# Two graph layers on one core: storing the zeros of the first sums in 13 parts beside the first table

## The chip, the cores and the metric

The kernel runs on one core of a Trainium2 chip. The metric is device time in microseconds (us) of one execution; the time before is the median of 9 runs. The engines have short names: PE is TensorE (PEld its weight loads), DVE is VectorE, ACT is ScalarE, POOL is GpSimd, SP is SyncE. SP, ACT and POOL also issue DMAs; "ACTq" and "SPq" in the views are such issues.

## The reference, cut to what matters

There are 6250 nodes of 256 features and 100,000 edges sorted by destination. Four layers follow one another, each on the normalised output of the one before, each added to it:

```python
x = x + gat_gat(_layernorm(x), src, dst, ...)     # two attention layers over the edges
x = x + experts_top2(_layernorm(x), ...)          # 8 experts, two for each node
x = x + mean_of_neighbours(_layernorm(x), ...)    # weighted mean over the edges, then an MLP
x = x + experts_routed(_layernorm(x), ...)        # 8 experts, routed once for all nodes
```

Only the beginning is changed. The first attention layer needs, for every node, a table row of `z = _layernorm(x) @ W1` (two heads of 128) with the scores `el` and `er`; messages `z[src]`, weighted by a softmax over the edges of a destination, are then added up for each destination.

## The kernel before, in words

**Stages.** The first stage is the pool `g1` (lines 1145 to 1184). It makes `table1` (6250 rows of 262 numbers) and the lists of edges. The second stage (`gat_edges`, from line 1232) gathers rows of `table1` by edge and adds them up, 50 tiles of 125 nodes one after another. Between the two lies `gat_general` (line 1185), a loop for oversized tiles that runs zero times here, but whose entry every engine passes before the second stage begins.

**What runs in the first stage.** Three jobs are mixed, each instruction placed on its engine's queue by a scheduler when the program is built; an engine then executes its queue strictly in order.

- *Edge ranges* (`edge_ranges`): where each tile's edges begin. It is one long chain of small steps, most of them on DVE, with three round trips to memory by indirect DMAs on POOL: `part` (L177), `win` (L220, three) and `orec`/`ow` (L293, eight). It ends with `starts` (L383).
- *Edge lists* (`edge_lists`): seven groups of up to eight tiles. For each group SP loads `raw` (L460) and POOL loads `wraw` (L463), addressed by `starts`; DVE, ACT and PE turn them (L467 to L499), and SP stores `dl_d` (L480) and `run_d` (L495). `raw` and `wraw` have two buffers.
- *The table*: 13 blocks of four tiles (the last of two). For each block ACT issues the load of `xb` (L1153); DVE normalises it (`normalize`, L508 to L513); PE turns it (L523) and ACT empties that into `xT` (L524); for each of the four tiles PE multiplies by `wl` into one bank `pz` (L1164), ACT copies 256 columns of it into `rows` (L1168) and DVE the other four (L1171); DVE copies `er` out (L1172); ACT issues two stores to `table1` (`store_tiles`, L1106). `xb` has three buffers, `rows` and `pz` two each.

At the end `item_lists` (L413 to L433) makes the lists that the loop of `gat_general` would use: five rounds of two wide products on PE, DVE work between them, two small stores each.

**The zeros.** `sums1` (6528 rows of 258 numbers) must be zero before the second stage adds to it. `clear(nc.sync, sums1, 0, 1)` at L1183 does it in one DMA on SP's queue, from a tile of zeros; the scheduler places it early, as L1120 of the profile. The first reader of `sums1` in the second stage is L745, then L663.

Of the kernel before, what the change touches and what calls it, by code (L numbers as in the profile page):

```python
# [13 lines left out]
F32 = mybir.dt.float32  # L14
# [4 lines left out]
OP = mybir.AluOpType  # L19
# [8 lines left out]
P = 128  # L28
NP = 125
D = 256  # L30
# [4 lines left out]
TB = 4  # L35
# [9 lines left out]
def network(ctx: ExitStack, tc: tile.TileContext, a, out, n_nodes: int, n_edges: int):  # L45


    nc = tc.nc
# [7 lines left out]
    blocks = [(t, min(TB, NT - t)) for t in range(0, NT, TB)]  # L56
# [445 lines left out]
    def normalize(pool, outs, ins, keep=None):  # L502

        n, p = len(ins), ins[0].shape[0]
        mv = keep if keep is not None else pool.tile([P, TB, 2], F32, name="mv")
        for j, x in enumerate(ins):
            st = pool.tile([P, 6], F32, name="st", bufs=4)
            nc.vector.bn_stats(st[:p], x)  # L508
            nc.vector.bn_aggr(mv[:p, j, :], st[:p])
        nc.scalar.activation(mv[:p, :n, 1:2], mv[:p, :n, 1:2], AF.Sqrt, bias=eps[:p])  # L510
        nc.vector.reciprocal(mv[:p, :n, 1:2], mv[:p, :n, 1:2])
        for j, (o, x) in enumerate(zip(outs, ins)):
            nc.vector.tensor_scalar(  # L513
                o, x, mv[:p, j, 0:1], mv[:p, j, 1:2], op0=OP.subtract, op1=OP.mult
            )

    def transpose_to(xT, ps, ins, func=AF.Copy):

        n, q = len(ins), ins[0].shape[0]
        for k in range(KD):  # L520
            pt = ps.tile([P, TB, P], F32, name="pt")
            for j, x in enumerate(ins):
                nc.tensor.transpose(pt[:, j, :q], x[:, k * P : (k + 1) * P], identf[:q, :q])  # L523
            nc.scalar.activation(  # L524
                xT[:, k, : n * q].rearrange("p (j q) -> p j q", q=q), pt[:, :n, :q], func
            )


    def gat_width(H):
        return H * (D // H + 1)  # L530

    def gat_weights(pool, W, al, ar, H):

        d = D // H
        wl = pool.tile([P, KD, D + 2 * H], F32, name="wl")
        nc.sync.dma_start(wl[:, :, 0:D], W.rearrange("(k p) f -> p k f", p=P))
        for s, v in enumerate((al, ar)):
            vb = row_to_all(pool, v, f"vb{s}")
            for h in range(H):
                for k in range(KD):  # L540
                    pr = pool.tile([P, D], F32, name="pr", bufs=2)
                    nc.vector.tensor_mul(pr[:, :d], wl[:, k, h * d : (h + 1) * d], vb[:, h * d : (h + 1) * d])
                    nc.vector.tensor_reduce(
                        wl[:, k, D + s * H + h : D + s * H + h + 1], pr[:, :d], AX.X, OP.add
                    )
        return wl
# [550 lines left out]
    def tiles_of(src, t0, n):  # L1097

        w = src.shape[1]
        return bass.AP(tensor=src.tensor, offset=src.offset + t0 * NP * w, ap=[[w, P], [NP * w, n], [1, w]])  # L1100

    def store_tiles(queue, dst, t0, n, v):

        to = dst[t0 * NP : (t0 + n) * NP, :].rearrange("(j p) w -> p j w", p=NP)
        for q in (slice(0, NP // 16 * 16), slice(NP // 16 * 16, NP)):
            queue.dma_start(to[q], v[q])  # L1106
# [7 lines left out]
    def clear(queue, acc, part, parts):  # L1114

        w = acc.shape[1]
        step = -(-NS // parts)
        lo, hi = part * step, min(NS, (part + 1) * step)
        if lo < hi:
            queue.dma_start(  # L1120
                acc[:, :].rearrange("(p j) w -> p j w", p=P)[:, lo:hi, :],
                blank[:, 0:w].unsqueeze(1).to_broadcast([P, hi - lo, w]),
            )
# [12 lines left out]
    x5_d = dram.tile([NT * NP, D], F32, name="x5_d")  # L1136
    uv_d = dram.tile([NT * NP, 2 * D], F32, name="uv_d")
    x6_d = dram.tile([NT * NP, D], F32, name="x6_d")
    NS = -(-(NT * NP + 2 * P) // P)
    sums1 = dram.tile([NS * P, gat_width(2)], F32, name="sums1")  # L1140
    sums2 = dram.tile([NS * P, gat_width(1)], F32, name="sums2")
    sums3 = dram.tile([NS * P, D + 1], F32, name="sums3")


    with tc.tile_pool(name="g1w", bufs=1) as wpool, tc.tile_pool(name="g1", bufs=2) as work, tc.tile_pool(
        name="g1p", bufs=2, space=PSUM
    ) as ps:
        edge_ranges()
        edge_lists()
        wl = gat_weights(wpool, a["L0_gnn_W1"], a["L0_gnn_al1"], a["L0_gnn_ar1"], 2)  # L1150
        for t0, n in blocks:
            xb = work.tile([P, TB, D], F32, name="xb", bufs=3)
            nc.scalar.dma_start(xb[:, :n, :], tiles_of(a["x"], t0, n))  # L1153
            xb = xb[:NP]
            normalize(work, [xb[:, j, :] for j in range(n)], [xb[:, j, :] for j in range(n)])
            xT = work.tile([P, KD, TB * NP], F32, name="xT")
            transpose_to(xT, ps, [xb[:, j, :] for j in range(n)])
            rows = work.tile([NP, TB, D + 6], F32, name="rows")
            heads = rows[:, :, 0 : D + 2].rearrange("p j (h f) -> p j h f", h=2)
            nc.vector.memset(heads[:, :, :, 0:1], 1.0)  # L1160
            for j in range(n):
                pz = ps.tile([P, 512], F32, name="pz")
                for k in range(KD):
                    nc.tensor.matmul(  # L1164
                        pz[:NP, : D + 4], xT[:, k, j * NP : (j + 1) * NP], wl[:, k, :],
                        start=(k == 0), stop=(k == KD - 1),
                    )
                nc.scalar.copy(  # L1168
                    heads[:, j, :, 1:], pz[:NP, 0:D].rearrange("p (h f) -> p h f", h=2)
                )  # L1170
                nc.vector.tensor_copy(rows[:, j, D + 2 :], pz[:NP, D : D + 4])  # L1171
            nc.vector.tensor_copy(er1[:NP, t0 : t0 + n, :], rows[:, :n, D + 4 :])  # L1172
            store_tiles(nc.scalar, table1, t0, n, rows[:, :n, :])
        none = wpool.tile([NT + 1, 2 * P], BF16, name="none")
        nc.vector.memset(none, 0.0)
        for v, k in ((er1_d, 6), (er2_d, 3)):
            nc.sync.dma_start(
                v[:, :, CH:, :].rearrange("t k c e -> t k (c e)"),
                none.unsqueeze(1).to_broadcast([NT + 1, k, 2 * P]),
            )  # L1180
        nc.sync.dma_start(x2_d[NT * NP :, :], blank[: P - NP, 0:D])
        nc.sync.dma_start(table3[NT * NP :, :], blank[: P - NP, 0 : D + 1])
        clear(nc.sync, sums1, 0, 1)  # L1183
        item_lists()
    gat_general(2, table1, er1, sums1, m_all)

# [188 lines left out]
    with tc.tile_pool(name="f1w", bufs=1) as wpool, tc.tile_pool(name="f1x", bufs=3) as work, tc.tile_pool(  # L1375
        name="f1p", bufs=2, space=PSUM
# [17 lines left out]
        rows = wpool.tile([P, NC, 2], I32, name="rows")  # L1394
# [43 lines left out]
        p = ps.tile([P, 512], F32, name="py")  # L1438
# [3 lines left out]
        p = ps.tile([P, 512], F32, name="py")  # L1442
# [88 lines left out]
    with tc.tile_pool(name="f1c", bufs=2) as work:  # L1531
        for t0 in range(0, NT, TL):
            lo = t0 * NP
# [7 lines left out]
            rows = work.tile([NP, TL, D + 1], F32, name="rows")  # L1541
# [491 lines left out]
    with tc.tile_pool(name="f3w", bufs=1) as wpool, tc.tile_pool(name="f3", bufs=1) as work, tc.tile_pool(  # L2033
        name="f3p", bufs=1, space=PSUM
# [51 lines left out]
```

## Time and profile before

| | |
|---|---|
| median of 9 runs | 4089.5 us (4085.39 to 4093.61) |
| the profiled execution: its own time, its span | 4091.05 us, 4089.4 us |
| first work of the second stage (ACT L844) | 171.83 us |
| busy in the span: PE, DVE, ACT, POOL | 2875.1, 2503.9, 952.3, 2601.1 us |
| DMA traffic in the span | 586.96 MB |
| `sums1` zeros, one DMA | 6579 KB |

A line of the timeline gives the start, the duration, the engine, the line of the kernel, the operation and its tiles, and in brackets how long the engine had stood idle before it and what released it. A line of the view of waits gives who waited, for whom, the sum, the number of times and the longest. In the table by stretches, after the busy time of each engine (with the count of instructions) come the granted PE clock, the mean busy share of the 16 DMA engines, and the GB/s they moved.

### The profile page before, as it was taken

The page shows a single profiled execution, that of the slowest core. Times are in us where ns is not written, and L with a number is a line of the kernel's source. Part 1 is how long each engine was busy: PE and PEld are TensorE (multiplying, and loading weights), DVE is VectorE, ACT ScalarE, POOL GpSimd, SP SyncE. Part 2 cuts the span into 40 slices and gives each one's busy share as a digit, 9 for nine tenths or more (in the row PEclk, how much of TensorE's full clock was granted, in tenths as well). Part 3 has the DMA queues.
Part 4 walks back from the last instruction along what each step waited for, and adds up shares of the span by engine and source line. Part 5 has one row for each costly group of instructions (what it writes and reads, how often), then busy time and mean ns, then how long its engine had stood idle before and what let it go on. Part 6 is the DMA issues. An engine that isn't in the chain of part 4 may idle for free. (4 is left out here: it accounts for less than half of the span.)

```text
span 4089.4 us, 38097 instructions
## 1 busy us (share of the span) xinstructions
PE 2875.1 (70%) x11159; PEld 2012.4 (49%) x11159; DVE 2503.9 (61%) x5186; ACT 952.3 (23%) x1774; POOL 2601.1 (64%) x2719
## 2 busy tenths in 40 slices
PE   5556566666563666767766789994287889888877
PEld 3334444444441444444444457773144667666656
DVE  5576666666654677777777633335544566656667
ACT  1222222222221222222222122221001122212223
POOL 2477777777756777777777234441377777777750
PEclk8777777777775788888888789997567999899998
DMA  7455555555535655555555231115645444544475
GB/s 164 125 154 156 155 156 157 155 156 155 156 102 152 164 164 164 163 164 161 164 159 160 74 137 65 64 65 168 187 110 161 133 138 133 155 135 139 133 184 158
DMA packets 319715, 586.96 MB, mean 144 GB/s; under 512 B 64363, under 2 KB 208932, under 8 KB 319245
## 3 DMA queue, kind: packets, MB, share of 16 engines
q0 software_dynamic: 129104, 351.03, 31.5%
q1 hardware_dynamic: 172868, 216.08, 18.6%
q10 hardware_dynamic: 17529, 17.31, 1.4%
q8 instruction: 96, 1.57, 0.2%
q14 instruction: 118, 0.97, 0.1%
HBM read 486.15 MB, written 98.05 MB: 143 GB/s over the span
## 5 line engine op out<-in xcount | busy, mean ns | idle before, releaser
L755 POOL DMA_INDIRECT z<-table,src_all x2412 | 2340.1, 970 | 864.1 <-issue 798.7
L946 PE MATMUL pacc<-z,wt 128*125 128x258 f32 (+1 forms) x3216 | 962.2, 449 | 21.1 <-DVE old L956 18.3
L946 PEld LDWEIGHTS pacc<-z,wt 128*125 128x125 f32 x3216 | 686.3, 224 | 179.6 <-issue 27.9
L1075 PE MATMUL pacc<-z,wt 128*125 128x257 f32 x1608 | 465.2, 431 | 111.8 <-DMA z<-table,src_all 104.2
L895 PE MATMUL pq<-identf,el 128*34 128x128 f32 (+1 forms) x306 | 79.4, 394 | 647.6 <-ACT el L888 515.6
L1075 PEld LDWEIGHTS pacc<-z,wt 128*125 128x125 f32 x1608 | 306.8, 204 | 256.8 <-DMA z<-table,src_all 207.6
L765 DVE TENSOR_TENSOR oh<-iota_b,px 128x2000 bf16<-128x2000 bf16 x153 | 339.7, 2220 | 126.5 <-ACT px L1047 126.4
L862 ACT CAST e<-pe 6x1536 bf16<-6x1536 f32 (+1 forms) x204 | 203.4, 997 | 740.2 <-PE pe L858 740.0
L895 PEld LDWEIGHTS pq<-identf,el 128*34 128x34 f32 (+1 forms) x306 | 26.7, 113 | 698.2 <-ACT el L888 604.8
L934 DVE TENSOR_TENSOR z<-z,pq 128x1032 f32<-128x1032 f32 (+1 forms) x202 | 233.6, 1218 | 187.8 <-PE pq L918 178.6
L846 DVE TENSOR_TENSOR own<-dr,px 125x2048 bf16<-125x2048 bf16 x102 | 232.7, 2281 | 23.0 <-ACT px L844 13.0
L858 PE MATMUL pe<-own,ek 125*6 125x512 bf16 (+1 forms) x408 | 154.3, 471 | 120.2 <-DVE own L846 84.8
L1512 POOL DMA_INDIRECT y_d<-y,r x105 | 104.3, 994 | 198.0 <-DVE r L1456 171.2
L1482 PE MATMUL ph<-w,xT 128*128 x420 | 201.2, 602 | 13.4 <-DVE xT L1471 7.3
L1506 PE MATMUL py<-w,hT 128*128 x840 | 198.5, 379 | 0.0
L1761 PE MATMUL pt<-x6T,w1f 128*128 128x250 f32 x800 | 184.1, 388 | 17.0 <-ACT hT L1767 17.0
L888 ACT COPY el<-z 128x32 f32<-128x32 f32 (+2 forms) x102 | 23.6, 231 | 701.1 <-DMA z<-table,src_all 655.6
L899 DVE TENSOR_TENSOR_SCAN f<-mask,pq 34x384 f32<-34x384 bf16 (+1 forms) x100 | 93.7, 937 | 137.4 <-PE pq L895 137.3
L1761 PEld LDWEIGHTS pt<-x6T,w1f 128*128 128x128 f32 x800 | 157.7, 200 | 39.2 <-ACT hT L1767 20.9
L1506 PEld LDWEIGHTS py<-w,hT 128*128 128x128 f32 x840 | 151.5, 190 | 16.3
L1487 DVE TENSOR_TENSOR h<-ph,b 128x512 f32<-128x512 f32 x105 | 72.6, 691 | 135.6 <-PE ph L1482 115.9
L1776 PE MATMUL py<-w2f,hT 128*125 128x256 f32 x608 | 146.5, 403 | 0.0
(500 smaller groups left out, 4033.3 us busy)
## 6 DMA issues: line engine op xcount, KB each, us to landing
dr<-dl_d SPq DMA_DIRECT2D x102, 512.0 KB
z<-table,src_all POOLq DMA_INDIRECT x2412, 2.8
sums<-blank SPq DMA_DIRECT2D x16, 771.0 KB
uv_d<-uv SPq DMA_DIRECT2D x19, 448.0 KB
z<-uv_d SPq DMA_DIRECT2D x7, 1120.0 KB
old<-sums SPq DMA_DIRECT2D x13, 514.0 KB
sums<-blank SPq DMA_DIRECT2D x1, 6579.0 KB
old<-sums SPq DMA_DIRECT2D x10, 645.0 KB
```

The costliest lines, as they stand in the source:

```text
L755: nc.gpsimd.indirect_dma_start(out=z[:, c, :], out_offset=None, in_=table[:, :], in_offset=bass.IndirectOffsetOnAxis(ap=src_all[:, i : i + ...
L765: nc.vector.tensor_tensor(oh[:, c0:c1], iota_b[:, 0:NP].unsqueeze(1).to_broadcast([P, n, NP]), px[:, c0:c1].unsqueeze(2).to_broadcast([P, ...
L846: nc.vector.tensor_tensor(own, s["dr"][:NP], px[:NP, X : X + 1].to_broadcast([NP, CH * P]), OP.is_equal)
L858: nc.tensor.matmul(pe[:, c - lo : c - lo + n], ek[:, NT if t == OVER else t].rearrange("p i h -> p (i h)"), s["own"][:, c : c + n], start= ...
L862: nc.scalar.copy(s["e6"][:, lo:hi], pe[:, 0 : hi - lo])
L934: nc.vector.tensor_tensor(zz, zz, x.unsqueeze(2).to_broadcast([P, n, d + 1]), OP.mult)
L946: nc.tensor.matmul(s["pacc"][:NP, 0:w], s["wt"][:, c, :], s["z"][:, c, 0:w], start=(c == 0), stop=(c == n - 1),)
L1075: nc.tensor.matmul(pacc[:NP, 0:w], s["wt"][:, c, :], s["z"][:, c, :], start=(c == 0), stop=(c == chunks(t) - 1),)
L1482: nc.tensor.matmul(ph, v["xT"][:, k, :], w1[:, v["one"], k, :].rearrange("p o f -> p (o f)"), start=(k == 0), stop=(k == KD - 1),)
L1506: nc.tensor.matmul(py[:, :D], v["hT"][:, f, :], w2[:, v["one"], f, :].rearrange("p o f -> p (o f)"), start=(f == 0), stop=(f == KF - 1),)
L1761: nc.tensor.matmul(ph[:, g * W : (g + 1) * W], x["w1"][:, s, k, f * P : (f + 1) * P], xT[:, k, :], start=(k == 0), stop=(k == KD - 1),)
L1776: nc.tensor.matmul(py[:NP, s, :], hT[:, s * KF + f, :], x["w2"][:, s, f, :], start=(f == 0), stop=(f == KF - 1),)
```

## The change

The one DMA that stores zeros to all of `sums1` is taken out. In its place each of the 13 blocks makes a small tile of zeros on DVE (`zeros`, 48 partitions of 258, as `x < x` on the block's first finished rows, so it cannot be made before them) and issues from ACT one DMA that stores it over 11 row positions of each of 48 partitions (4 in the last block). ACT, no longer DVE, copies the last four columns of each `pz`. Buffers: `xb` 5 instead of 3, `rows` 3 instead of 2, `pz` 3 instead of 2.

```diff
+    ZP = 48
     NS = -(-(NT * NP + 2 * P) // P)
+    assert NS * P % ZP == 0
...
-            xb = work.tile([P, TB, D], F32, name="xb", bufs=3)
+            xb = work.tile([P, TB, D], F32, name="xb", bufs=5)
...
-            rows = work.tile([NP, TB, D + 6], F32, name="rows")
+            rows = work.tile([NP, TB, D + 6], F32, name="rows", bufs=3)
...
-                pz = ps.tile([P, 512], F32, name="pz")
+                pz = ps.tile([P, 512], F32, name="pz", bufs=3)
...
-                nc.vector.tensor_copy(rows[:, j, D + 2 :], pz[:NP, D : D + 4])
+                nc.scalar.copy(rows[:, j, D + 2 :], pz[:NP, D : D + 4])
             nc.vector.tensor_copy(er1[:NP, t0 : t0 + n, :], rows[:, :n, D + 4 :])
             store_tiles(nc.scalar, table1, t0, n, rows[:, :n, :])
+
+            zeros = work.tile([ZP, gat_width(2)], F32, name="zeros")
+            some = rows[:ZP].rearrange("p j w -> p (j w)")[:, 0 : gat_width(2)]
+            nc.vector.tensor_tensor(zeros, some, some, OP.is_lt)
+            part = -(-(NS * P // ZP) // len(blocks))
+            lo, hi = t0 // TB * part, min(NS * P // ZP, (t0 // TB + 1) * part)
+            nc.scalar.dma_start(
+                sums1[:, :].rearrange("(p j) w -> p j w", p=ZP)[:, lo:hi, :],
+                zeros.unsqueeze(1).to_broadcast([ZP, hi - lo, gat_width(2)]),
+            )
...
-        clear(nc.sync, sums1, 0, 1)
```

## The prediction

> **What bounds the kernel now.** I read the busy time by stretches first, cut at the two places where the first stage changes its nature: 87 us, where SP loads the first `raw`, and 143 us, where the last group of edges is done.
>
> ```profile
> 0.00:87.00 87.00, 40.59 (x151) 28.33 (x151) 47.52 (x273) 13.54 (x32) 13.96 (x25) 0.84 0.73 168
> 87.00:143.00 56.00, 42.63 (x175) 33.37 (x175) 34.46 (x179) 19.63 (x61) 24.88 (x50) 0.79 0.53 131
> 143.00:172.00 29.00, 22.84 (x76) 10.20 (x76) 16.16 (x49) 6.92 (x20) 2.26 (x1) 0.88 0.23 66
> 172.00:4080.00 3908.00, 2769.00 (x10757) 1940.49 (x10757) 2403.80 (x4682) 912.00 (x1663) 2559.99 (x2643) 0.82 0.52 144
> ```
>
> Until 87 us no engine is busy much over half, but the DMA engines are at 0.73. From 87 to 143 us PE is busy 43 of 56 us, from 143 on 23 of 29. The change touches nothing behind 172 us, and there no engine waits for anything left over from before, so whatever the first stage gains or loses arrives at the end one for one.
>
> Next the timeline of DVE and SP, where the stage's beginning is held up:
>
> ```profile
> 11.13 0.65 SPq L1120 DMA_DIRECT2D sums<-blank  x1
> 16.77 28.33 SPq L1247 DMA_DIRECT2D y_d<-blank  x1
> 30.26 0.56 DVE L183 CAST pd<-part 50x782 f32<-50x782 int32 x1 [8.22 <-DMA part<-in_edges,row]
> 47.57 0.43 DVE L508 BATCH_NORM_STATS2 st<-xb 125x6 f32<-125x256 f32 x1 [7.03 <-DMA xb<-in_x]
> 48.58 0.34 DVE L226 CAST wd<-win 50x384 f32<-50x384 int32 x1
> 86.96 6.74 SPq L460 DMA_DIRECT2D raw<-in_edges  x11
> ```
>
> The zeros are issued at 11.13 us. Cut in tens, the DMA engines' share is 0.96, 1.07, 1.10 and 1.04 from 10 to 50 us. In this time the chain of the edge ranges makes its first two trips to memory: `part` lands 12.5 us after its issue, the three `win` 7.7 to 8.8 us. The eight gathers of the third trip, after the rush, land in 2.6 to 3.8 us. The 28.33 us of L1247 cost nothing: SP's next work is at 86.96.
>
> Last the waits of the whole stage (0 to 172 us), for the table's loop:
>
> ```profile
> ACT rows L1168 <- PE pz L1164: 53.6, 33, 6.4
> PEld pz L1164 <- DVE rows L1171: 23.3, 13, 6.3
> PE pz L1164 <- DVE rows L1171: 19.6, 8, 5.9
> DVE st L508 <- DMA xb<-in_x: 15.6, 5, 7.0
> ```
>
> PE waits 19.6 us for a `pz` bank whose last four columns DVE hasn't copied, because those copies (0.15 us each) stand in DVE's queue behind other work. Of this, 5.9 us lie in the wait for `xb` at 40.5 us.
>
> **The change part by part.** Its order of instructions, as built, I read beside that of before.
>
> *Taken from the early rush.* 6.7 MB leave the time from 11 to 48 us. `part` (313 KB) would land in 3 to 5 us instead of 12.5; DVE waited 8.22 for it. With five `xb` buffers two more blocks are loaded in the same time (1 MB, some 5 us at the 200 GB/s of 20 to 30 us), so I take 7.5 saved, between 4 and 8.2. The 7.03 us for `xb` go with the buffers. Next late is `win`: the last of its gathers is issued by 40.4 us, lands near 43.5 at the 2.6 to 3.8 us of the third trip, and L226 could follow 5 us before its 48.58: take 5, between 2 and 6. From there to the gathers at 63.70 DVE waited 1.20 and 2.33 us (a table store, and PE standing behind `pz` products at clock 0.50): take 3.5 saved, between -2 (in the new order L270 stands behind a product that waits for ACT's `xT`) and 4. The eight gathers and the last steps (21 us) are as before. Sum: 16 us (4 to 18); SP begins the lists near 71.
>
> *The edge lists*, 55.5 us before. In the new order 2.5 blocks are stored or nearly so when they begin and 6.4 when they end, against 3.3 and 9.4 before: 2.2 blocks fewer to work on beside them. A block costs PE 5.1 us at full clock (16 products at 0.25, 8 turns at 0.13, both from rows of 143 to 153 us), so up to 11 us; the floor is POOL's eight `wraw` issues per group (4.5 us, with 0.8 to 2.2 between). Against it, four parts of zeros (545 KB, 2.7 us each at 200 GB/s) now share the DMA engines with the `raw` loads, and SP stands when one is late: up to 11 us. I take 8 saved, between 14 saved and 4 lost.
>
> *The tail.* Now 6 blocks are left at its start instead of 3.1. Stores of blocks 10 and 11 were issued 6.83 us apart (145.05, 151.88), 2.27 us of it PE's wait for L1171, which goes. Without it 4.56; PE's own work is 5.1; ACT has 4.8 (four copies of 0.37, four new small ones of some 0.2 as for L844 and L888, two `xT` of 0.57, four DMA issues of 0.31 to 0.40). I take PE's 5.1: 2.9 blocks, 15 us more; between 13 and 20 (at 6.83). The item lists stand among these blocks, as before.
>
> *The end.* Before, the last store (`item_off`, 169.83) landed for 171.83. Now it is half a block of table, 256 KB, and 198 KB of zeros: 1 us more, 0 to 3. The zeros themselves are read first at 239.19 us (L745), so nothing else waits for them; if that cover of some 65 us were gone, the parts would cost their landing.
>
> *What is added to the engines.* DVE makes 13 tiles of zeros, at some 0.4 us each (nearest: 0.41 for L513), 5 us, and drops 50 copies, 7.3 us. ACT gains 50 small copies, 10 us, and 13 issues of 0.4, on 40 us busy of 172. Behind each issue of zeros on ACT stand the fourth tile's copies and the table stores; the issue waits for DVE's `zeros`, which waits for the first tile's copy. In the order as built DVE has at most four normalisations of 0.41 us ahead of it, and ACT two more tiles to copy meanwhile: I take nothing, bounds 0 and 2.3 us a part (PE's longest wait for L1171 in the tail).
>
> *One transfer in 13 parts.* The small gathers of the third trip answer in 2.6 to 3.8 us each, yet eight of them, issued 1.25 us apart, were through 12.3 us after the first issue: what a DMA costs beyond its bytes overlaps with its neighbours, and nobody stands at a part's landing. So I take no cost for the splitting. The Trainium skill speaks against such splitting: "DMA: Bandwidth & Descriptors", section "Bandwidth", has "Batch DMAs to ≥1 MiB for ≥75% of peak", and its section on the anatomy of a DMA puts a fixed cost of about 2 us on each. By that page 12 more DMAs would cost an estimated 24 us if each were waited for, and the change would end 16 us slower; no row here shows such a wait.
>
> Sum: -16 - 8 + 15 + 1 = -8 us. The span becomes 4081.4, the profiled time 1.65 above it 4083.05; the median lies 1.55 below the profiled execution, so 4081.5.
>
> **The rivals.** *Given back in the tail.* Blocks keep the measured pace of 6.83 us, since the new order splits a block's products in two halves around turns of the next block, so that three banks serve no better than two: 2.9 x 1.7 = 5 us lost of the 8, and with the early gain at 13 instead of 16 no change, -5 to +4, 4089.5. For it: the interval is a row, not a sum. Against it: the same interval holds the wait that is removed.
>
> *ScalarE stands behind the zeros: slower.* Ten of the parts are issued after 71 us. If DVE is behind (during edge groups, or in the item lists, where it waits for PE) and ACT stands 2.3 us at each, 23 us are lost, ending at -8 + 23 = +15, 4104.5. It decides from 0.8 us a part. For it: ACT already waited 1.3 us once for DVE's L1172, which stands in the same place of the loop. Against it: ACT is idle most of the stage, and its 53.6 us of waits are for PE.
>
> *The far end of the forecast.* The early gain at 18, the lists at 14, the tail at 13 and no landing: -19, 4070.5.
>
> **How the numbers follow.** About 0.2%, 8 us, is what a measurement of this kernel can tell from no change. The forecast has 0.50; its sum lies on that edge, and I give it 0.28 beyond and 0.22 within, since of PE's 19.6 us of waits for L1171 only the 5.9 and the 2.27 have gone into a term. Its far end has 0.15, all beyond. Given back has 0.11, all within. ScalarE behind the zeros has 0.24, all slower. So faster 0.43, same 0.33, slower 0.24. The forecast's own range is 4070 to 4088. For 8 in 10 I reach down to 4068 and up to 4098, which leaves out most of the slow rival (0.15) and little below.
>
> **What would show it.** Right: DVE's waits at L183 and before L226 shrink to a few us; SP's first `raw` at 67 to 76 us; the last edge group done by 115 to 124; no line of PE waiting for DVE's `rows`; ACT L844 near 163. The early part is wrong if `raw` still begins after 80. The tail is wrong if blocks store over 6.5 us apart without item lists between. The slow rival shows as ACT waiting for `zeros` by more than 8 us in all, or PE's waits for ACT grown by as much. If L844 comes early and the end does not, the later stages were not as independent as I hold them to be.

## The result and the profile after

Slower: 4114.8 us median of 11 runs (4102.89 to 4121.62), against 4088.8 for the kernel before in the 35 runs made beside them. The ratio is 1.0062, with a 95% interval of 1.0053 to 1.0071, or 26 us. The forecast was 4081.5, within 4068 to 4098. For eight rows of the table below, from "no parts" to "one late store, ACT", both kernels ran at a granted PE clock of about 0.77, where before itself took 4757 and 4765 us, nearly all of the increase behind the first stage and for a reason not looked into; their ratios are against these times.

The profiled execution took 4114.99 us and has a span of 4113.0, 23.6 more than before. First the busy time by stretches, cut where SP loads the first `raw`, where the last edge group is stored and where ACT makes its first copy of the second stage (after the busy times: PE clock, DMA share, GB/s):

```profile
0.00:73.60 73.60, 32.93 (x116) 23.07 (x117) 45.01 (x254) 10.47 (x32) 14.19 (x25) 0.78 0.38 109
73.60:133.10 59.50, 31.56 (x129) 24.11 (x128) 27.36 (x127) 15.89 (x61) 24.78 (x50) 0.73 0.58 127
133.10:197.50 64.40, 48.61 (x158) 29.37 (x158) 29.42 (x89) 19.54 (x71) 2.78 (x2) 0.74 0.58 129
197.50:4104.00 3906.50, 2764.28 (x10757) 1938.59 (x10757) 2402.54 (x4678) 910.66 (x1662) 2559.94 (x2643) 0.83 0.52 144
```

Before, the marks were 86.96, 142.77 and 173.13. So the beginning is 13.4 us shorter, the edge lists 3.6 longer (59.45 against 55.81), the tail 34.0 longer (64.40 against 30.36). Together that is +24.3, and from the last mark to the end both take 3916 us: the whole loss lies in the first stage.

The timeline of the changed kernel, first DVE and SP in the beginning:

```profile
22.64 0.56 DVE L183 CAST pd<-part 50x782 f32<-50x782 int32 x1 [0.56 <-DMA part<-in_edges,row]
37.52 0.35 DVE L226 CAST wd<-win 50x384 f32<-50x384 int32 x1 [4.83 <-DMA win<-in_edges,near]
73.61 10.53 SPq L460 DMA_DIRECT2D raw<-in_edges  x11
```

`part` is there 7.6 us earlier and `win` 11 us. But the eleven `raw` issues of the first group take 10.53 us where they took 6.74.

Then ACT and PE in the tail:

```profile
138.08 3.65 ACTq L1106 DMA_DIRECT2D table<-rows  x2
141.77 1.07 ACT L524 ACTIVATE xT<-pt 128x500 f32<-128x500 f32 x2 [3.72 <-issue]
142.39 1.02 PE L420 MATMUL p<-step,ones 50*1 50x512 f32 x2 [2.64 <-DVE step L418]
144.53 1.91 PE L420 MATMUL p<-step,ones 50*1 50x512 f32 x2
148.08 4.70 PE L1166 MATMUL pz<-wl,xT 128*125 128x260 f32 x10
153.58 3.61 ACTq L1106 DMA_DIRECT2D table<-rows  x2
160.32 1.50 PE L425 MATMUL p<-step,shift_held 50*1 50x512 f32 x2
161.75 4.70 PE L1166 MATMUL pz<-wl,xT 128*125 128x260 f32 x10
184.18 3.93 ACTq L1106 DMA_DIRECT2D table<-rows  x2
196.16 1.28 ACT L844 ACT_TABLE_LOAD   x1 [5.01 <-DMA sums<-zeros]
```

A pair of table stores, issued right behind a part of zeros, occupies ACT for 3.65 us; before, two such issues took 0.8. ACT's next work, the `xT` of the following block, stands 3.72 us behind that. PE idles 2.64 us here, but what releases it is DVE, with a step of the item lists (L418), not ACT.

PE's clock is then halved, from 143.66 to 153.90 us, although PE is busy all of that time: the second L420 pair takes 1.91 us instead of 1.02, and ten products 4.70 instead of 2.5. It is halved again from 160.73 to 167.56 us, and before this second fall PE had not idled more than 0.31 us at a time since 153.8. What went before it, without a break from 155.49 on, were twelve products of the item lists (L420 and L425), each with a single column of weights (the `50*1` in the line). In the run with the first six parts, where these products lie two or four at a time between the table's products, the clock is 1.00 from 152 to 188 us. The second profile of the changed kernel has both falls within 0.2 us of these times.

The waits of the stage (0 to 197 us):

```profile
ACT sf L467 <- DMA raw<-in_edges: 17.9, 5, 5.7
DVE df L469 <- DMA raw<-in_edges: 15.0, 5, 5.6
PE pz L1166 <- ACT xT L524: 10.2, 10, 2.1
ACT xT L524 <- issue: 9.5, 3, 3.7
ACT sf L467 <- DMA wraw<-in_edge_weight: 7.7, 1, 7.7
```

No line has PE waiting for DVE's `rows` any more (19.6 us before). In its place PE waits 10.2 us for ACT's `xT` (0.7 before), ACT 9.5 us at issues, and the lists wait for their own loads.

### The profile page after: what moved, and what is told of

Read it like the earlier page. It is cut to its first block, busy times and chain, and to the rows that moved or that the text cites. A ratio compares the mean times of both kernels' runs of the same rounds, so it can differ in the third digit from the quotient of the medians.

```text
span 4113.0 us, 38167 instructions
## 1 busy us (share of the span) xinstructions
PE 2877.4 (70%) x11159; PEld 2015.1 (49%) x11159; DVE 2505.8 (61%) x5149; ACT 956.6 (23%) x1824; POOL 2601.7 (63%) x2719
## 5 line engine op out<-in xcount | busy, mean ns | idle before, releaser
L946 PEld LDWEIGHTS pacc<-z,wt 128*125 128x125 f32 x3216 | 683.2, 224 | 176.4 <-issue 28.1
L888 ACT COPY el<-z 128x32 f32<-128x32 f32 (+2 forms) x102 | 23.6, 232 | 735.0 <-DMA z<-table,src_all 701.1
```

The lines of the kernel that those rows point to most:

```text
L946: nc.tensor.matmul(s["pacc"][:NP, 0:w], s["wt"][:, c, :], s["z"][:, c, 0:w], start=(c == 0), stop=(c == n - 1),)
```

## The experiments

The stretches of the first stage can be compared over all of them; "start" is ACT's first copy of the second stage, and all numbers but the ratio come from one profile each.

| run | first raw | lists | tail | start | ratio (95%) |
|---|---|---|---|---|---|
| before | 86.96 | 55.8 | 30.4 | 173.1 | |
| before again | 93.79 | 56.6 | 29.2 | 179.6 | |
| after | 73.61 | 59.5 | 64.4 | 197.5 | 1.0062 (1.0053 to 1.0071) |
| after again | 73.99 | 59.2 | 64.4 | 197.6 | |
| no parts | 89.96 | 55.9 | 30.3 | 176.1 | 1.0027 (0.9995 to 1.0059) |
| parts only | 72.96 | 61.6 | 57.7 | 192.3 | 1.0045 (1.0019 to 1.0071) |
| one late store, SP | 73.94 | 55.3 | 68.2 | 197.5 | 1.0088 (1.0047 to 1.0129) |
| small parts | 76.28 | 56.7 | 73.2 | 206.2 | 1.0070 (1.0041 to 1.0100) |
| parts on POOL | 74.85 | 59.6 | 57.8 | 192.2 | 1.0030 (1.0005 to 1.0054) |
| halves | 87.19 | 57.5 | 39.4 | 184.1 | 1.0000 (0.9966 to 1.0034) |
| before with halves | 86.48 | 56.1 | 50.1 | 192.7 | 1.0008 (0.9981 to 1.0034) |
| one late store, ACT | 75.81 | 57.9 | 65.0 | 198.7 | |
| tail parts | 95.89 | 56.5 | 33.1 | 185.6 | 1.0029 (1.0015 to 1.0044) |
| list parts | 80.90 | 59.6 | 55.4 | 195.9 | 1.0048 (1.0034 to 1.0062) |
| first six parts | 84.69 | 60.1 | 47.4 | 192.3 | 1.0048 (1.0032 to 1.0065) |
| POOL, iota early | 76.93 | 61.1 | 42.7 | 180.8 | 1.0015 (1.0002 to 1.0027) |
| before, iota early | 93.39 | 57.0 | 28.1 | 178.5 | 0.9998 (0.9986 to 1.0010) |
| nine parts, POOL | 75.04 | 55.9 | 37.8 | 168.8 | 1.0000 (0.9990 to 1.0010) |

**How far single profiles can be trusted.** Both kernels once more, unchanged.

> The kernel before once more, for a second profile: how far the marks of its first stage differ between two executions. If marks can be compared within 2 us, SP's first raw is at 85 to 89, the last edge group at 141 to 145 and the second stage's start at 171 to 175 us. If they differ by 5 us or more, the stretches between marks are compared and not the marks.

> The changed kernel once more, for a second profile: lists of 58 to 61 us, a tail of 60 to 65 us and pairs of table stores at 1.6 to 3.9 us in it, if the first profile was typical of it.

The changed kernel repeats to 0.4 us. Before does not; its second profile has these lines of SP and ACT:

```profile
49.94 0.33 DVE L226 CAST wd<-win 50x384 f32<-50x384 int32 x1
93.79 6.23 SPq L460 DMA_DIRECT2D raw<-in_edges  x10
179.55 0.17 ACT L844 COPY px<-dl_all 128x16 f32<-128x16 f32 x1
```

Its first `raw` came 6.8 us later than in the first profile, while lists (56.6) and tail (29.2) agree within 1.2 us. Only 1.4 us of this had been lost by L226 (49.94 against 48.58), in the rush of the zeros. By the gathers on POOL it was 3.2 (66.91 against 63.70), and the rest was lost behind 80 us, where PE's granted clock was 0.97 in the first profile and 0.50 in the second:

```profile
80.00:87.00 7.00, 5.94 (x33) 3.79 (x32) 4.79 (x28) 1.23 (x3) 0.00 (x0) 0.97 0.45 128
80.00:87.00 7.00, 7.00 (x27) 5.12 (x26) 2.76 (x17) 1.33 (x3) 0.00 (x0) 0.50 0.28 75
```

So stretches are compared here. The early gain of the change is between 13 and 20 us, and what differs between these two is in part PE's clock.

**The parts undone.** The change with its parts taken out:

```diff
-            zeros = work.tile([ZP, gat_width(2)], F32, name="zeros")
...
+        clear(nc.sync, sums1, 0, 1)
```

> The changed kernel with its 13 parts undone: all zeros leave in one store on SP at the start, as before; ScalarE empties the products alone and the extra buffers stay. If the parts cost the time (bytes beside the edge lists, or ScalarE standing at their issue), the loss of 26 us goes: SP's first raw is back between 80 and 87 us, five table blocks are stored before the lists and about eleven when they end, so the second stage begins 5 to 15 us earlier than before and the time is 4070 to 4088. If emptying and buffers cost it (split products, blocks held up by ScalarE), the time stays at 4105 or above.

Lists and tail are those of before (55.9, 30.3), so the parts are what costs, be it directly or by the other order of instructions that is built with them. But emptying by ACT and the buffers brought nothing either. PE waits for ACT where it waited for DVE:

```profile
PE pz L1166 <- ACT xT L524: 9.0, 8, 3.0
PE pz L1166 <- ACT rows L1173: 8.8, 3, 6.5
```

That is 17.8 us against the 19.6 that went. `raw` was not earlier than in before: the expected 4070 to 4088 missed, since there was no gain to add.

**The parts alone.** The kernel before, with the parts of the change and nothing else of it.

```diff
+            zeros = work.tile([ZP, gat_width(2)], F32, name="zeros")
...
-        clear(nc.sync, sums1, 0, 1)
```

> The kernel before with the 13 parts alone: VectorE still copies the last four columns, and there are three xb, two rows and two pz. If the parts cost the time, 4105 to 4120, with raw near 74 us, lists of 58 us or more and a tail of 50 us or more (about 7 of 13 blocks are stored when the lists end). If emptying and buffers cost it, the early gain is left alone: 4070 to 4080.

Lists 61.6, tail 57.7, slower than before: the parts alone bring a loss. But the issues behind them hardly stand in this tail. Two parts, each with the pair of table stores that follows it:

```profile
145.78 0.33 ACTq L1182 DMA_DIRECT2D sums<-zeros  x1
151.39 0.83 ACTq L1106 DMA_DIRECT2D table<-rows  x2
173.99 0.33 ACTq L1182 DMA_DIRECT2D sums<-zeros  x1
176.52 1.66 ACTq L1106 DMA_DIRECT2D table<-rows  x2
```

Here the pairs come 2.5 to 5.6 us behind their part, the last one excepted, where in the changed kernel they come 0.4 to 2.6 us behind it. The seven pairs take 7.7 us in all, against 19.5 there. The tail is long all the same, 10 us longer than with the first six parts only, though as many blocks are left at its start as in the changed kernel and the clock is 0.91. So a tail with parts in it can be long without much standing of ACT.

**One late store, on SP.** Parts out; one DMA of all zeros, made from the last block's rows:

```diff
+            if t0 // TB == 12:
+                zeros = lists.tile([ZP, gat_width(2)], F32, name="zeros")
...
+                nc.sync.dma_start(
+                    sums1[:, :].rearrange("(p j) w -> p j w", p=ZP),
+                    zeros.unsqueeze(1).to_broadcast([ZP, NS * P // ZP, gat_width(2)]),
+                )
```

> The changed kernel without the parts: one store of all zeros on SP, made from the last block's rows, so that it leaves only at the end of the first stage. ScalarE's instructions stand in the same order as in the kernel with the parts undone. If the bytes beside loads are what costs, here neither the early loads nor the lists have them: raw at 72 to 76 us as with the parts, lists of 52 to 56 us, five blocks stored before and eleven after, the second stage 15 to 25 us earlier than before, and 4065 to 4078 if the 6.7 MB (33 us at 200 GB/s) are hidden under the second stage's start, up to 4100 if they hold up its gathers. If emptying and buffers cost the time, above 4100.

With no zeros beside them, early loads and lists are as hoped (73.94, 55.3), and the last block was stored at 140.7 us. Then SP's timeline:

```profile
143.11 0.72 SPq L1180 DMA_DIRECT2D sums<-zeros  x1
143.93 36.12 SPq L433 DMA_DIRECT2D item_off<-to  x1
```

The next issue, a store of 2 KB, stands 36.12 us on the queue. The expected 4065 to 4100 failed by that: what is issued on the same queue behind a DMA of 6.7 MB waits for most of it. The rest was still under way: the DMA engines' share was 0.60 from 180 to 185 us.

**Small parts.** Thirteen issues on ACT, 50 KB each instead of 545; the rest in one late store on SP.

```diff
-                sums1[:, :].rearrange("(p j) w -> p j w", p=ZP)[:, lo:hi, :],
+                sums1[:, :].rearrange("(p j) w -> p j w", p=ZP)[:, lo : lo + 1, :],
```

> The changed kernel with its 13 parts on ScalarE cut from 545 to 50 KB each; the rest leaves in one store on SP at the end of the stage. If the bytes of the parts cost the time (raw loads and table stores land late), it comes near the kernel with one late store, 4065 to 4085. If it is ScalarE that stands at 13 more issues, whatever they carry, raw is near 74 us but the tail stays above 45 us and the time at 4100 to 4115.

Lists 56.7 us and pairs of table stores at 0.80 to 0.83 in the tail: thirteen issues cost nothing when they carry little. The time is lost to the late store, for which ACT waited 56.6 us.

**Parts on POOL.** The queue alone is changed.

```diff
-            nc.scalar.dma_start(
+            nc.gpsimd.dma_start(
                 sums1[:, :].rearrange("(p j) w -> p j w", p=ZP)[:, lo:hi, :],
```

> The changed kernel with its 13 parts issued on POOL's queue: same bytes, same pace, same parts, but no part stands in ScalarE's queue. If the price is ScalarE standing at its issues (the table stores' pair at 1.6 to 3.9 us instead of 0.8), the pairs are back at 0.8 to 0.9, the tail from the last edge group to the second stage falls from 62 to 35 us or less, and the time is within 6 us of before. If the price is the bytes themselves beside raw loads and table stores, the lists take 58 us or more, the tail 50 us or more, and it stays 15 to 30 us slower than before.

This missed, and told most. The timeline of ACT and POOL:

```profile
141.32 3.12 ACTq L1106 DMA_DIRECT2D table<-rows  x2
146.69 3.09 ACTq L1106 DMA_DIRECT2D table<-rows  x2
142.11 0.70 POOL L1182 DMA_DIRECT2D sums<-zeros  x1 [4.41 <-DVE rows L1162]
164.81 2.28 POOL L413 IOTA ii<- 50x2560 int32 x1
```

ACT's pairs stand 3.1 us although no part is in its queue. So in this run an issue stands while parts from another queue are in flight (the DMA engines' share was 0.91 from 134 to 151 us). It is not always so: with the parts on POOL and the iota early, below, the pairs take 0.80 to 0.87 us. Standing alone did not slow the blocks: with no item lists among them they were stored at 136.21, 141.32, 146.69 and 150.76. The stage was late because the item lists' iota stood on POOL behind the last parts until 164.81. The lists took 59.6 us with five blocks stored beside them, and 59.5 in the changed kernel with four. Without big parts beside them it is six blocks in before and seven in several runs, at 55.3 to 57.9 us: how many blocks lie beside the lists does not set their length.

**Zeros in halves.** Half at once on SP, half late on ACT, with and without the rest of the change.

```diff
+        nc.sync.dma_start(
+            sums1[:, :].rearrange("(p j) w -> p j w", p=ZP)[:, :68, :],
...
+            if t0 // TB == 12:
...
+                nc.scalar.dma_start(
+                    sums1[:, :].rearrange("(p j) w -> p j w", p=ZP)[:, 68:, :],
```

> Emptying by ScalarE and the buffers as in the change, but the zeros in two stores: half at once on SP as before, half on ScalarE's queue behind the last table store but one, made from the last block's rows. If what the 13 parts cost is their place (beside the edge lists, ahead of table stores in one queue) and the first rush charges 13 us for all of the zeros, raw is at 78 to 83 us, the lists take 55 to 57 us, the second half (16 us at 200 GB/s) lies beside the item lists, the second stage begins 4 to 12 us earlier than before, and so does the end: ratio 0.997 to 0.999. If the second half is waited for by SP or at the stage's end, no change or up to 10 us slower.

> The kernel before with the zeros in the same two halves and nothing else changed (VectorE copies, old buffers). If emptying and buffers are worth nothing, it does as the halves with them: raw at 77 to 82 us, ratio 0.997 to 0.999. If they are worth the 5 to 10 us that the forecast gave them, it is that much behind.

No gain: half the bytes delayed `part` no less than all of them did (DVE L183 at 33.66 in both, 30.26 in before), and the late half made SP's item stores stand 2.3 and 3.2 us, or, in the second run, ACT's last table stores 17.5 us. The two do not differ beyond their intervals.

**One late store, on ACT's queue.** As the late store on SP, but:

```diff
-                nc.sync.dma_start(
+                nc.scalar.dma_start(
```

> The one late store of all zeros, this time on ScalarE's queue behind the last table store but one, not on SP's among the item lists. If the 36.1 us that SP stood behind the late store was its own queue being full, SP's item stores go on and only the landing (33 us from about 142 us) sets the second stage's start: ScalarE's first copy of it at 176 to 183 us, against 197.5 with the store on SP. If SP stood for the bytes of memory or for the engines, it stands again and the start stays at 190 us or later.

SP's item stores now went on, two of them at 2.2 and 3.3 us and none at 36, so the 36 us were the queue's. The start was missed: issued at 147.56, the store would have had to land by 181, but the second stage began at 198.66. The DMA engines' share was still 0.84 from 170 to 180 us and 0.66 from 180 to 190; that the start waited for the landing is likely, not shown.

**Parts beside the last four blocks only.** The other 99 of 136 rows of each partition go at once on SP. The order on PE is that of the kernel without parts for the first 320 instructions of this stage, and another from there on.

```diff
+            if t0 // TB >= 9:
+                zeros = work.tile([ZP, gat_width(2)], F32, name="zeros")
...
+        nc.sync.dma_start(
+            sums1[:, :].rearrange("(p j) w -> p j w", p=ZP)[:, :99, :],
```

> ScalarE empties and the buffers are there, as in the kernel without parts, and each engine has that kernel's order of instructions; new are only four parts of zeros on ScalarE's queue beside the last four blocks (37 of 136 rows for each partition), while the other 99 leave at once on SP. If ScalarE stands at the table stores behind a part, the pairs take 1.6 to 3.9 us there instead of 0.8, the tail is 8 to 16 us longer than the 30.3 us without parts, and the second stage begins at 182 to 192 us. If the tail of the changed kernel is long by its order alone, the tail stays at 28 to 33 us and the pairs at 0.8.

Pairs of 3.34 and 4.47 us, yet the tail is 33.1 us, only 2.9 longer than without parts. One of the four parts lies beside the lists. With some three blocks left, PE is busy 24.7 of these 33.1 us: the item lists run on meanwhile (last store at 180.41), and ACT then waits 4.9 us for the last part to land.

**Parts beside the first nine blocks only**, in the changed kernel's order; the other 37 rows go at once on SP.

```diff
+            if t0 // TB < 9:
```

> The changed kernel with its order of instructions kept, but the parts of the last four blocks (37 of 136 rows) leave at once on SP instead; the first nine parts stay on ScalarE. If ScalarE's standing and the last landing make the tail, it shrinks from 62.5 to 48 to 53 us (four pairs of stores back at 0.8 to 0.9 us, no landing of 5 us at the end). If the order makes it (six and a half blocks left at its start, item lists in their midst), it stays at 57 us or more. The early gain falls to some 5 us, since a quarter of the zeros is ahead of the first loads.

The tail is 55.4 us, between the two: 9.0 off with four parts less. The order on PE is that of the changed kernel for the first 112 of the tail's 158 instructions, and by there 2.3 us are saved. The other 6.7 come in the last four blocks, which have no parts here, and also another order.

**Parts beside the first six blocks only.**

```diff
+            if t0 // TB < 6:
```

> The changed kernel with the parts of the first six blocks alone on ScalarE, the other 70 of 136 rows at once on SP: the order of instructions stays that of the change up to the end of the lists, six blocks stored, and no part stands in the tail. If blocks left over (6.5 instead of 3.3, 5 us each) are what the order costs, the tail is 45 to 50 us against 30 without parts and 62.5 with all, so the order has some 16 us of it and the parts 14. If the parts in ScalarE's queue make the tail, it is 30 to 38 us. In the lists, 55.5 to 57 us if only parts beside them cost, since then half are gone.

The tail's stretch, and two lines of ACT in it:

```profile
144.80:192.30 47.50, 40.14 (x158) 25.20 (x158) 26.49 (x82) 19.75 (x71) 2.78 (x2) 0.90 0.37 103
150.82 0.83 ACTq L1106 DMA_DIRECT2D table<-rows  x2
183.34 0.83 ACTq L1106 DMA_DIRECT2D table<-rows  x2
```

The tail has the same 158 PE instructions as in the changed kernel, every pair at 0.8, the clock at 0.90 instead of 0.74, PE busy 40.1 instead of 48.6 us. So the blocks left at its start make 47.4 us without parts. The other 17.0 come with the parts and with the order that is built with them: up to the end of the lists the two kernels' order is the same, but in the tail it differs from PE's 23rd instruction on, and here the item lists are spread among the blocks. The lists did not shorten with half of the parts gone; the four that start beside them are enough.

**POOL with the iota early, and its control.** The item lists' iota is made ahead of the loop; in the control it is the only edit to before.

```diff
+        ii = wpool.tile([NT, IW], I32, name="ii")
+        nc.gpsimd.iota(ii, pattern=[[1, IW]], base=0, channel_multiplier=0)
```

> The parts on POOL's queue as in the earlier run, and the iota that the item lists begin with is made at the start instead of on POOL behind the last parts. If only that iota kept the item lists waiting in the earlier run (134 to 165 us), they now run beside the last blocks: the second stage begins at 163 to 174 us instead of 192, with the bytes of the zeros still paced through the lists, and the time is 0 to 10 us below before. If the bytes or the landing of the last parts hold the stage, it begins at 180 us or later and is slower than before.

> The kernel before with the item lists' iota made at the start and nothing else: the control for the run with the parts on POOL. In before the iota runs 2.5 us after the last edge group and takes 2.3 us, so 0 to 5 us are to be had: second stage at 168 to 173 us, ratio 0.999 to 1.000.

The control shows no change. With the parts on POOL the tail fell from 57.8 to 42.7 us, so the iota had cost some 15. What is left is likely the landing of the last part, since the DMA engines' share falls to nothing by 176 us:

```profile
170.56 0.60 POOL L1182 DMA_DIRECT2D sums<-zeros  x1 [0.84 <-DVEq L649]
180.77 0.17 ACT L842 COPY px<-dl_all 128x16 f32<-128x16 f32 x1
```

**Nine parts on POOL.** The version the runs pointed to: parts of 16 rows beside the first nine blocks.

```diff
+            if t0 // TB < 9:
+                part = -(-(NS * P // ZP) // 9)
...
+                nc.gpsimd.dma_start(
```

> The version that the runs point to: nine parts of 16 rows on POOL's queue beside the first nine blocks, so that none is behind the last ones, and the item lists' iota at the start. The early gain stays (raw 74 to 78 us), nothing stands in ScalarE's queue, nine or more blocks are stored when the lists end (134 to 139 us), and the last part has landed before the last block is done, so that the second stage begins at 164 to 170 us instead of 173: 3 to 9 us below before, ratio 0.998 to 0.9993. If the bytes beside the lists or POOL's queue take more than that back, it is no faster.

The second stage begins at 168.75 us, 4 to 11 before the two profiles of before, and the lists took 55.9, with two of these parts beside them, nearly as many bytes as three of 11 rows. But the last three parts left only at 137.97, 141.72 and 156.02, and ACT's pairs beside them took 3.58 and 4.18 us. Over 12 runs there is no difference from before: 4 to 11 us would be 0.1 to 0.3%, the interval reaches 0.1% to each side, and the gain at the start is not seen in the times. No version here beats it.

## Why the prediction was wrong

*The early gain, 16 us (4 to 18).* Right in size: 13.4 us between the first profiles; against the second profile of before, with its slower PE clock, 20.2. `raw` was at 73.61, inside the 67 to 76 named.

*Emptying by ACT.* Right that PE's waits for DVE's `rows` vanish, wrong that this is worth anything: without parts, 17.8 us of waits for ACT stand in place of 19.6, and the tail is 30.3 us. The forecast took it as pace in the tail.

*The edge lists, 8 us saved.* This step failed: 3.6 us were lost, a miss of 11.6. Both of its halves went. The blocks beside the lists are not what paces them: with four or five blocks stored beside them they took 59.2 to 61.6 us, with six (before) or seven (four runs with no parts there) 55.3 to 57.9. What the longer lists have in common is three or four parts of 545 KB issued beside them, at some 4 us. The waits for the loads of `raw` and `wraw` go with it, 33 to 58 us in all in three profiles with the parts, 6 to 25 in three without. That the bytes are the cause is not shown: the two parts of 16 rows on POOL, nearly as many bytes as three of 11 rows, were beside lists of 55.9 us. The prediction had the sharing with the `raw` loads as an opposing term of up to 11 us, and weighed it too low.

*The tail, 15 us, and the end, 1.* As far as the number of blocks left goes, this was right: with no parts in the tail it is 47.4 us against 30.4, 17.0 where 16 was said. But the sum took PE's 5.1 us a block at full clock, with the item lists among the blocks as before, and in the changed kernel that failed: three of the five rounds of the item lists stand in a row, and PE's clock is halved for long stretches. Blocks with no item lists between stored 5.0 to 6.2 us apart, as said.

*The issues of parts on ACT, taken at nothing (0 to 2.3 us a part).* This step failed. It priced the wrong wait, ACT waiting for the tile `zeros`; of that the trace has no line. What stands is the issue behind the part. The six pairs in the tail take 18.7 us where they would take 5.0, 2.3 us a pair; that the bound of the wrong wait is met is chance. What counts is how soon the next issue comes: each of these pairs began 0.4 to 2.6 us behind its part and was through 4.0 to 5.2 us behind it, while pairs that began 3.7 us or more behind theirs, in the run with the parts only, took 0.83 to 1.05 us.

The 17.0 us by which the changed kernel's tail is longer than that of the first six parts, row by row up to the last product (57.6 against 41.0 us): PE is busy 48.6 us against 40.1 for the same 158 instructions, at a granted clock of 0.77 against 0.92, which makes 8.5. PE waits for ACT's `xT` and `rows` 6.9 us against 1.6, 5.3 more. It waits 2.9 us for DVE's steps of the item lists, against none. The last 0.3 lie behind the last product. So the standing of ACT accounts for some 5 of the 17 us. Half of them is the slower clock, and whether that comes of the parts or only of where the item lists fall is open: no run has the changed kernel's order without its parts.

A row of the profile before had the standing. The issue of `y_d`, behind the 6.7 MB of zeros, took 28.33 us on SP's queue. The prediction read it as costing nothing, since SP had no work then. A part is 532 of its 6579 KB in the view of DMA issues, so its share is 28.33 x 532 / 6579 = 2.3 us, at each of 13 places where ACT has work, if an issue follows at once.

*One transfer in 13 parts.* The price was not a fixed cost of each: in the run with small parts, thirteen issues of 50 KB cost nothing visible. The rule of the Trainium skill, "DMA: Bandwidth & Descriptors", section "Bandwidth", to batch DMAs to 1 MiB or more, had the right sign here by luck: parts of 545 KB cost time and parts of 50 KB, further below that size, did not. The fixed cost of about 2 us that the prediction took from the same page stands there for DMAs issued by POOL; the parts were issued by ACT. The advice in "Perfetto Trace Analysis", section "DMA Optimizations", is to balance DMAs over the engines that can issue them if generating descriptors is the bottleneck. Moving the parts to POOL's queue left ACT's pairs at 3.1 us in one run and at 0.80 to 0.87 in the other, with the iota early, and the ratio went from 1.0062 to 1.0030 and 1.0015; how much of that is the queue and how much the order is not separated.

In sum, from the forecast's -8 us to the measured +24.3 at the second stage's start: early +2.6, lists +11.6, blocks left and end of the tail +1, and 17.0 more in the tail (slower clock 8.5, waits for ACT 5.3, for DVE 2.9, end 0.3). The rival "ScalarE stands behind the zeros" was nearest, by its place on ACT and its sign, not by its mechanism.

## What to carry to other kernels

A big store that nobody reads is not free where it is issued: an issue close behind it on the same queue stood until most of its bytes were through (36 us behind 6.7 MB), and in several runs one on another queue stood too, for 2 to 4 us. An issue that left some 4 us behind a part of 545 KB took its usual time. Look in the profile for issues that take many times their usual 0.3 us, ask what had been issued before, and scale that row to the place where the store is to go. Cover by "no work just then" does not move along. And before an engine's backlog is priced as pace, find the row that paces the stretch: the lists had theirs elsewhere, so taking work from beside them gave nothing. Last, read the new order for where the single-column products fall: in the changed kernel twelve of them in a row went ahead of a halved clock, and work priced at full clock cost nearly twice that.

## What the runs showed of the hardware

- A store of zeros holds up the loads behind it by its volume and, it seems, by how it is laid out: `part` was read (L183) at 22.64 us behind none, and behind stores from 48 partitions at 30.17 (1.8 MB), 33.66 (3.4 MB), 34.21 (3.5 MB) and 37.34 (4.9 MB). Behind 6.7 MB from 128 partitions it was read at 30.26.
- Two executions of the kernel before differ by 6.8 us at the first `raw`; of that, 1.4 us lie in the rush of the zeros and some 3.6 behind 80 us, where PE's granted clock was 0.97 in one and 0.50 in the other. Two of the changed kernel differ by 0.4.
- PE's granted clock was 0.50 from 143.66 to 153.90 us and from 160.73 to 167.56 in the changed kernel. The first fall came 1.3 us after an idle stretch of 2.64 us had ended; the second came with no idle stretch over 0.31 us in the 7 us before it, at the end of twelve products with a single column of weights. The Trainium skill, "TensorE: Matmul & The Clock Gate", Part 1, has the full clock back after some 3.4 us of sustained work. Here it came back 5.8 us after the wide products had begun (148.08 and 161.75), so if the page's rule holds, the products with one column did not count as such work; that is inferred.
